# Four small edits to a hand-listed four-layer graph kernel: a bank rule for the list, one elu, one graph's row sums, the last stores' queue

## The chip, the cores and the metric

The kernel runs on one core of a Trainium2 chip. The metric is the time of one execution on the device in microseconds (us); the median over several runs is compared. All times below are measured on that chip: run times, or times of one execution recorded by the hardware profiler, counted from the start of its span.

## What is computed

Four layers run one after the other over 32 graphs of 512 nodes with 128 features each, all in float32, with one 0/1 adjacency matrix `adj` for all graphs. Every layer adds its result to x:

```python
h = relu(layernorm(x)); x = x + layer(h)
# layer 0: an edge-weighted message layer
x_h = elu(h @ Wi + bi)
e   = sigmoid(x_h @ We[H:] (target) + x_h @ We[:H] (source) + be) * mask(adj)
recv = elu(concat(e @ x_h, x_h * sum(e, -1)) @ Wn + bn)
out  = concat(recv, x_h) @ Wm + bm
# layer 1: five gated steps
av = concat(adj @ h, adj @ h); u3 = h @ u3_w.T
z, r = sigmoid(av @ w3.T + u3), sigmoid(av @ w4.T + u3)
h = (1 - z) * h + z * tanh(av @ w5.T + (r * h) @ u5.T)
# layer 2: adj @ (h @ W) + b
# layer 3: sum over k of adj^k @ h @ V[k], k = 0..3 (the two stacks of powers use the same adj)
```

## The kernel before

**Tiles.** A graph's activations are one tile of 128 partitions x 512 float32. Slots are pooled by kind: 36 `f` tiles in SBUF, 4 `q` tiles (rounded float32r copies), 8 small `s` tiles, 5 `x` tiles of four graphs each, 8 PSUM banks `b`, and DRAM scratch tiles `m` and `d`. Engines are named as in the profile: PE (matmul), DVE (VectorE), ACT (ScalarE), POOL (GpSimd), SP (SyncE, which issues most transfers).

**The order is made in advance.** The kernel does not emit instructions as it describes them. Each piece of work is registered with `op(engine, us, due, emit, reads, writes, ...)` (class `Plan`), with an assumed duration, a due time and the values it reads and writes. `Plan.op` derives what must come before it: the writer of each value read, and, for a value written, its earlier readers. `Plan.order` then goes through assumed time and picks for each engine the ready operation with the earliest due time; this list becomes the program, every engine runs its own part strictly in order, and semaphores are placed afterwards from what the instructions really read and write. So an entry that is changed anywhere can shift the places of all later ones.

**Start.** The first 18 us of the list (`BRANCH`) load x and adj, build the mask and fill PE with otherwise idle matmuls on ones (L307). Then a check whether adj is exact in float32r is read by all engines (L996), and one of two arms of an If is taken (L997). With these inputs it is the arm that splits a value into a rounded high part and the rest (`parts`, L821 on ACT and L825 on DVE).

**Layer 0** (`layer0`) for graph b: layernorm (L481 to L501), a turn into feature rows (PE for the first four graphs, L378 and L574), the product with Wi (L449), `elu`, the messages and scores (`send` L593 on PE; `score` L600 on DVE and `take` L598 on ACT read the same bank), the targets spread over partitions (L630), four tanh of edges (L645, ACT), each multiplied with the mask (L648, DVE), four products (L656), the row sums, `own` (L687), the product with Wn, a second `elu` and the product with Wm (L697), then the addition to x (L469).

`elu` reads one PSUM bank three times: exp (L554) and tanh (L454) on ACT, and the relu, on ACT (L562) or, for the first two graphs, on DVE (L559). DVE joins them (L564, L566).

Row sums: graphs 0 and 1 add the four edge tiles in pairs on DVE (L664) and sum over partitions with two float32 products on PE. All other graphs add the four tiles by transfers: SP copies the first into `sums` (L671) and POOL issues three accumulating transfers (L674), each after the one before has landed. ACT rounds the sum (L678), DVE takes the rest (L679) and PE sums both (L684).

**Layer 1** steps turn their result by DVE (L390), a write to DRAM (L392) and a read back (L403), both issued by SP, then `parts` and the products with adj (L851). **Layer 3** runs once for four graphs (`layer3`, products L932 and L941); its last round adds to x (L953, DVE) and stores each quarter (L958, issued by SP). The last quarter of the last four graphs is written to `mask` (L963) and stored after the If has ended (L1003, SP).

Of the kernel before, what the change touches and what calls it, by code (L numbers as in the profile page):

```python
# [14 lines left out]
ALU = mybir.AluOpType  # L15
# [26 lines left out]
class Plan:  # L42
# [18 lines left out]
    def op(self, eng, us, due, emit, reads=(), writes=(), two=None, keep=0, result=None,  # L61
           earliest=0.0, margin=0.0):

        two = eng == "POOL" if two is None else two
        o = Op(eng, us, self.RESULT[eng] if result is None else result, emit, two, keep)
        o.earliest, o.margin = earliest, margin
        for v in reads:  # L70
            o.before.add(v.writer)
        for v in writes:
            o.before.update(v.readers)
            if v.writer:
                o.before.add(v.writer)
            elif v.kind and v.slot is None:
                o.takes.append(v)
        for v in reads:
            v.readers.append(o)
        for v in writes:  # L80
            v.writer, v.readers = o, []
        o.vals = [v.whole or v for v in dict.fromkeys([*reads, *writes])]
        for v in o.vals:
            v.left += 1
        for v in [*reads, *writes, *o.vals]:
            self.vals[v] = True
        o.before -= {o, None}
        o.due = max([due, *(b.due for b in o.before)])
        for b in o.before:
            b.after.append(o)  # L90
        self.ops.append(o)
# [125 lines left out]
def tile_four_graph_layers(  # L217
# [27 lines left out]
    nc = tc.nc  # L245
    B, N, D = x.shape
    NC = N // P
    G = 4
    NG = B // G
# [5 lines left out]
    MARGIN = 10.0  # L255
    FIRST = 2

    T_MM, T_TR, T_NARROW, T_PASS = 0.86, 0.44, 0.224, 0.23
    T_VEC, T_COPY, T_ACT, T_DMA = 0.61, 0.5, 0.6, 0.45
# [3 lines left out]
    op = plan.op  # L263
# [20 lines left out]
    def at(v):  # L284
        if v.tile is not None:
            return v.tile
        return places[v.kind][v.slot] if v.whole is None else at(v.whole)[:, v.part]
# [262 lines left out]
    def elu(p, bias, half, due, keep, scale=1.0, relu_by_vector=False):  # L550


        e, t, r = Val("f"), Val("f"), Val("f")
        op("ACT", T_ACT, due, lambda: nc.scalar.activation(  # L554
            at(e), at(p), AF.Exp, bias=at(bias), scale=scale), [p, bias], [e], keep=keep)
        tanh(t, p, due, half, scale / 2)
        if relu_by_vector:
            assert scale == 1.0
            op("DVE", T_VEC, due, lambda: nc.vector.tensor_scalar(  # L559
                at(r), at(p), at(bias), 0.0, op0=ALU.add, op1=ALU.max), [p, bias], [r])  # L560
        else:
            op("ACT", T_ACT, due, lambda: nc.scalar.activation(  # L562
                at(r), at(p), AF.Relu, bias=at(bias), scale=scale), [p, bias], [r])
        op("DVE", T_VEC, due, lambda: nc.vector.scalar_tensor_tensor(  # L564
            at(t), at(e), 1.0, at(t), op0=ALU.add, op1=ALU.mult), [e, t], [t], two=True)
        op("DVE", T_VEC, due, lambda: nc.vector.scalar_tensor_tensor(  # L566
            at(r), at(t), 0.0, at(r), op0=ALU.min, op1=ALU.add), [t, r], [r], two=True)
        return r

    def layer0(b, h, due):  # L570
# [5 lines left out]
        else:  # L576
# [2 lines left out]
        pace = 0.6 if b < FIRST else 1.0  # L579
        d = due + 6 * pace  # L580
        xhT = elu(product(Wi_sb, hT, d, blocks=b >= G), bi_sb, bi_half, d, KEEP,
                  relu_by_vector=b < FIRST)

        d = due + 14 * pace
        msg, ends = Val("f"), Val("s")
# [22 lines left out]
        d = due + 20 * pace  # L608
# [33 lines left out]
        es = []  # L642
        for jc in range(NC):
            e = Val("f")
# [8 lines left out]
        d = due + 30 * pace  # L653
# [6 lines left out]
        if b < 2:  # L660
            ps = Val("b")
            pair = [Val("f"), Val("f")]
            for i in range(2):
                op("DVE", T_VEC, d - 6, lambda i=i: nc.vector.tensor_tensor(  # L664
                    at(pair[i]), at(es[2 * i]), at(es[2 * i + 1]), op=ALU.add),
                    [es[2 * i], es[2 * i + 1]], [pair[i]], two=True)
            for i in range(2):
                product(ones, pair[i], d - 1, ps, start=i == 0, stop=i == 1)
        else:
            sums = [Val("f")]  # L670
            op("SP", T_DMA, d - 10, lambda: nc.sync.dma_start(at(sums[0]), at(es[0])),  # L671
               [es[0]], [sums[0]], result=2.6)
            for e in es[1:]:
                op("POOL", 1.0, d - 10, lambda e=e: nc.gpsimd.dma_start(  # L674
                    at(sums[0]), at(e), accum_op=ALU.add), [e, sums[0]], [sums[0]],
                   two=False, result=4.6)
            high, low, ps = Val("q"), Val("q"), Val("b")
            op("ACT", T_COPY, d, lambda: nc.scalar.copy(at(high), at(sums[0])), [sums[0]], [high])  # L678
            op("DVE", T_VEC, d, lambda: nc.vector.tensor_tensor(  # L679
                at(low), at(sums[0]), at(high).bitcast(F32), op=ALU.subtract),  # L680
                [sums[0], high], [low], two=True)
            def total():
                for n, part in enumerate((low, high)):
                    nc.tensor.matmul(at(ps), at(ones_r), at(part), start=n == 0, stop=n == 1)  # L684
            op("PE", 2 * T_PASS, d, total, [high, low, ones_r], [ps])
# [6 lines left out]
        d = due + 44 * pace  # L692
# [43 lines left out]
    def list_rest(exact, pool):  # L736
        n = 25 if exact else 16
# [185 lines left out]
        def layer3(g, hT, due, pace):  # L923
            z = None
            for k in (3, 2, 1, 0):
                new = []
                for ic in range(NC):
                    d = due + ((3 - k) * NC + ic) * pace
                    pz = Val("b")
                    def start(pz=pz, k=k, ic=ic, last=z is None):  # L930
                        for i in range(G):
                            nc.tensor.matmul(  # L932
                                at(pz)[:, ts(i, D)], at(hT[i])[:, ts(ic, P)], at(V[k]),
                                start=i == 0, stop=last and i == G - 1,
                            )
                    op("PE", G * T_NARROW, d, start, [*hT, V[k]], [pz])
                    if z is not None:
                        for jc in range(NC):
                            def add(pz=pz, ic=ic, jc=jc, z=z[jc]):
                                for n, part in enumerate(z):  # L940
                                    nc.tensor.matmul(  # L941
                                        at(pz), at(adjT)[:, jc, ts(ic, P)], at(part),
                                        start=False, stop=jc == NC - 1 and n == PARTS - 1,
                                    )
                            op("PE", PARTS * T_ADJ, d, add, [*z[jc], adjT], [pz])
                    if k:
                        new.append(parts(pz, d))
                        continue
                    xv = X[g * G : (g + 1) * G]
                    def x_part(ic=ic):  # L950
                        return at(X_group[g])[:, :, ic, :]
                    def finish(pz=pz, x_part=x_part):
                        nc.vector.tensor_tensor(  # L953
                            x_part(), x_part(), at(pz).rearrange("p (b d) -> p b d", b=G),
                            op=ALU.add,
                        )
                    def store(ic=ic, x_part=x_part):
                        nc.sync.dma_start(  # L958
                            out[g * G : (g + 1) * G, ts(ic, P), :].rearrange("b p d -> p b d"),
                            x_part(),  # L960
                        )
                    if g == NG - 1 and ic == NC - 1:
                        op("DVE", T_VEC, d, lambda pz=pz, x_part=x_part: nc.vector.tensor_tensor(  # L963
                            at(mask)[:, 0, :].rearrange("p (b d) -> p b d", b=G), x_part(),
                            at(pz).rearrange("p (b d) -> p b d", b=G), op=ALU.add),
                            [pz, *xv], [mask])
                        continue
                    chunk = Val(whole=X_group[g])
                    op("DVE", T_VEC, d, finish, [pz, *xv], [chunk])

                    op("SP", 0.5, d, store, [chunk], margin=(NC - 1 - ic) * 2.7 + (g < NG - 1) * MARGIN)
                z = new


# [66 lines left out]
```

## Time and profile before

| what | us |
| --- | --- |
| runs | 1671.55, 1669.9, 1669.99; median 1669.99 |
| the profiled execution, own time | 1671.54 |
| its span, first to last instruction | 1669.4 |
| PE busy in the span | 1655.4 (99%) |
| DVE busy | 1428.0 (86%) |
| ACT busy | 1130.5 (68%) |
| POOL busy | 243.0 (15%) |

The busy time of PE counts overlapping matmuls once, and the ends of matmuls are modelled, so short gaps may be hidden in it. A graph's own path is long, but many graphs are under way at once: what counts is whether PE has something to do. The page shows PE at nine tenths or more in all of forty slices but the second and the last.

### The profile page before, as it was taken

To read this page: it belongs to the slowest core of one execution; us is meant where nothing else is said; L and a number is where in the kernel's file an instruction comes from. 1 tells how busy PE (TensorE), PEld (TensorE's weight loads), DVE (VectorE), ACT (ScalarE), POOL (GpSimd) and SP (SyncE) were. 2 spreads that over 40 slices of the span, in tenths; PEclk is the share of its full clock that TensorE was granted. 3 is DMA by queue.
4 is the path that set the end of the run, shared out by engine and by line. 5 is a ranking of instruction groups with operands and counts; after the bars stand their busy time and mean duration, and the time that the engine had idled before them with its cause. 6 is when DMAs were issued, how large, how long until landed. Compare 5 with 4: busy or idle time off the path is not lost.

```text
span 1669.4 us, 21469 instructions
## 1 busy us (share of the span) xinstructions
PE 1655.4 (99%) x6585; PEld 1072.9 (64%) x6585; DVE 1428.0 (86%) x3341; ACT 1130.5 (68%) x2133; POOL 243.0 (15%) x243
## 2 busy tenths in 40 slices
PE   9899999999999999999999999999999999999998
PEld 6555555656666666666666666666666666666787
DVE  8889999999998888889988898888999888877842
ACT  7876777877766677666667677676778666655640
POOL 2311101211111111111111111101121110000100
PEclk9999999999999999999999999999999999999999
DMA  3554524543445443454434454444454443222202
GB/s 98 128 121 127 151 88 123 147 123 110 136 111 145 117 115 103 107 148 122 121 112 108 121 139 115 114 113 126 128 140 127 127 122 100 89 64 87 84 14 59
DMA packets 285501, 189.10 MB, mean 113 GB/s; under 512 B 77376, under 2 KB 238016, under 8 KB 285376
## 3 DMA queue, kind: packets, MB, share of 16 engines
q1 hardware_dynamic: 272416, 164.03, 33.3%
q0 software_dynamic: 12960, 23.60, 8.5%
q8 instruction: 54, 0.88, 0.2%
q14 instruction: 71, 0.58, 0.1%
HBM read 82.78 MB, written 73.33 MB: 94 GB/s over the span
## 4 chain that ended last, share of the span: by engine, by line
PE 96%; DMA 1%; ACT 1%; DVE 1%; issue 0%; SPq 0%; DVEq 0%; ACTq 0%
PE b L449 44%; PE b L851 21%; PE b L941 11%; PE b L932 7%; PE b L656 6%; PE b L697 3%; PE b L914 2%; PE b L593 1%; PE b L684 1%; DMA f<-m 1%; ACT f L495 0%; PE b L307 0%; DMA f<-in_adj_dram 0%; DMA m<-f 0%; PE b L378 0%
## 5 line engine op out<-in xcount | busy, mean ns | idle before, releaser
L438 ACT COPY f<-b 128x512 f32<-128x512 f32 x356 | 206.6, 586 | 146.4 <-PE b L851 94.3
L851 PE MATMUL b<-AQ,r 128*128 128x512 f32 x1024 | 303.7, 438 | 0.0
L486 POOL TENSOR_TENSOR s<-s,nhalf 128x4 f32<-128x4 f32 x128 | 156.4, 1222 | 869.5 <-DVE s L484 793.0
L851 PEld LDWEIGHTS b<-AQ,r 128*128 128x128 f32 x1024 | 192.1, 188 | 89.2 <-issue 51.7
L876 DVE TENSOR_TENSOR f<-f,b 128x512 f32<-128x512 f32 x320 | 211.9, 676 | 25.5 <-PE b L449 23.3
L390 DVE STREAM_TRANSPOSE f<-f 128x512 f32<-128x512 f32 x246 | 207.3, 846 | 27.6 <-ACT f L495 27.1
L941 PE MATMUL b<-r,A_r 128*128 128x512 f32 x768 | 223.6, 426 | 0.0
L454 ACT ACTIVATE f<-f,b4w 128x512 f32<-128x512 f32 x160 | 115.0, 722 | 152.8 <-DVE f L876 152.4
L495 ACT ACTIVATE f<-x,s 128x128 f32<-128x128 f32 x504 | 206.9, 488 | 13.8 <-DVE s L490 13.4
L941 PEld LDWEIGHTS b<-r,A_r 128*128 128x128 f32 x768 | 139.0, 189 | 45.6 <-issue 23.4
L449 PE MATMUL b<-f,u3T 128*128 128x512 f32 x320 | 163.3, 592 | 2.4 <-DVE f L897 2.4
L449 PE MATMUL b<-f,u5T 128*128 128x512 f32 x320 | 162.9, 592 | 0.0
L449 PE MATMUL b<-f,w4T 128*128 128x512 f32 x320 | 162.9, 592 | 0.0
L449 PE MATMUL b<-f,w5T 128*128 128x512 f32 x320 | 162.7, 592 | 0.0
L449 PE MATMUL b<-f,w3T 128*128 128x512 f32 x320 | 162.2, 592 | 0.0
L674 POOL DMA_DIRECT2D f<-f x90 | 80.6, 896 | 486.9 <-DMA f<-f 94.6
L454 ACT ACTIVATE f<-b,b5w 128x512 f32<-128x512 f32 x160 | 109.7, 686 | 56.7 <-PE b L449 55.7
L851 PE MATMUL b<-A_r,r 128*128 128x512 f32 x512 | 147.5, 430 | 0.1
L893 DVE TENSOR_TENSOR f<-f,f 128x512 f32<-128x512 f32 x160 | 109.2, 683 | 43.0 <-ACT f L454 42.4
L932 PEld LDWEIGHTS b<-V,f 128*128 128x128 f32 x1024 | 131.1, 191 | 23.2 <-issue 17.7
L825 DVE TENSOR_TENSOR r<-f,r 128x512 fp32r<-128x512 f32 x192 | 130.4, 681 | 5.9 <-ACT r L821 5.9
L932 PE MATMUL b<-V,f 128*128 128x128 f32 x1024 | 133.1, 275 | 0.0
(111 smaller groups left out, 2526.2 us busy)
## 6 DMA issues: line engine op xcount, KB each, us to landing
m<-f SPq DMA_DIRECT2D x246, 256.0 KB, 2.1
f<-m SPq DMA_DIRECT2D x186, 256.0 KB, 3.0
f<-f POOLq DMA_DIRECT2D x90, 256.0 KB, 3.7
f<-m SPq DMA_DIRECT2D x240, 64.0 KB, 2.5
x<-in_x_dram SPq DMA_DIRECT2D x32, 256.0 KB, 3.3
out_dram<-x SPq DMA_DIRECT2D x31, 256.0 KB, 2.7
f<-f SPq DMA_DIRECT2D x30, 256.0 KB, 2.4
f<-d SPq DMA_DIRECT2D x28, 256.0 KB, 5.1
```

Of the source, the lines that this page charges most:

```text
L390: op("DVE", us, due, lambda: nc.vector.transpose(view_out(at(blocks)), view_in(at(src))), [src], [blocks])
L438: op("ACT", us, due, lambda: nc.scalar.copy(at(t), at(src)), [src], [t])
L449: nc.tensor.matmul(to, at(w), of, start=start, stop=stop)
L454: op("ACT", us, due, lambda: nc.scalar.activation(at(dst), at(src), AF.Tanh, bias=at(bias), scale=scale), [src, bias], [dst])
L486: op("POOL", 1.35, due, lambda: nc.gpsimd.tensor_tensor(stat(SCALE), stat(VAR), at(neg_half), op=ALU.pow), [s, neg_half], [s])
L495: nc.scalar.activation(at(h)[:, ts(c, P)], at(X[b])[:, c, :], AF.Relu, bias=stat(SHIFT)[:, c : c + 1], scale=stat(SCALE)[:, c : c + 1],)
L825: op("DVE", T_VEC, due, lambda: nc.vector.tensor_tensor(part(lo), whole(), part(hi).bitcast(F32), op=ALU.subtract), [src, hi], [lo], two=two)
L851: nc.tensor.matmul(at(pa), at(part)[:, ts(jc, P)], view(at(columns)[:, jc, :]), start=jc == n == 0, stop=jc == NC - 1 and n == PARTS - 1,)
L876: op("DVE", T_VEC, d, lambda: nc.vector.tensor_tensor(at(s), at(u), at(pg), op=ALU.add), [u, pg], [s])
L893: op("DVE", T_VEC, d, lambda c=c, h=h: nc.vector.tensor_tensor(at(c), at(c), at(h), op=ALU.subtract), [c, h], [c], two=True)
L932: nc.tensor.matmul(at(pz)[:, ts(i, D)], at(hT[i])[:, ts(ic, P)], at(V[k]), start=i == 0, stop=last and i == G - 1,)
L941: nc.tensor.matmul(at(pz), at(adjT)[:, jc, ts(ic, P)], at(part), start=False, stop=jc == NC - 1 and n == PARTS - 1,)
```

## The change

Four edits. (1) In `Plan.op`, an operation that reads a PSUM bank is also listed after the last earlier reader of the bank if that reader is on another engine. (2) The first `elu` takes its relu on ACT for all graphs. (3) The third graph (b = 2) adds its four edge tiles by three DVE additions in place of one SP and three POOL transfers. (4) The stores of the last four graphs' first three quarters are issued from ACT's queue. Two lines are added near the top, so the changed kernel's line numbers are 2 higher from there on and 8 or 9 higher after `layer0`'s sums (L851 becomes L859, L958 becomes L967).

```diff
@@ class Plan, op
         for v in reads:
             o.before.add(v.writer)
+            if v.kind == "b" and v.readers and v.readers[-1].eng != eng:
+                o.before.add(v.readers[-1])
         for v in writes:
@@ layer0
         xhT = elu(product(Wi_sb, hT, d, blocks=b >= G), bi_sb, bi_half, d, KEEP,
-                  relu_by_vector=b < FIRST)
+                  relu_by_vector=False)
@@ layer0, row sums of graphs 2 and up
             sums = [Val("f")]
-            op("SP", T_DMA, d - 10, lambda: nc.sync.dma_start(at(sums[0]), at(es[0])),
-               [es[0]], [sums[0]], result=2.6)
-            for e in es[1:]:
-                op("POOL", 1.0, d - 10, lambda e=e: nc.gpsimd.dma_start(
-                    at(sums[0]), at(e), accum_op=ALU.add), [e, sums[0]], [sums[0]],
-                   two=False, result=4.6)
+            if b < 3:
+                for n in range(1, NC):
+                    op("DVE", T_VEC, d - 10, lambda n=n: nc.vector.tensor_tensor(
+                        at(sums[0]), at(es[0] if n == 1 else sums[0]), at(es[n]), op=ALU.add),
+                        [es[n], es[0] if n == 1 else sums[0]], [sums[0]], two=True)
+            else:
+                ...
@@ layer3, last round
-                        nc.sync.dma_start(
+
+                        (nc.scalar if g == NG - 1 else nc.sync).dma_start(
                             out[g * G : (g + 1) * G, ts(ic, P), :].rearrange("b p d -> p b d"),
                             x_part(),
                         )
@@
-                    op("SP", 0.5, d, store, [chunk], margin=(NC - 1 - ic) * 2.7 + (g < NG - 1) * MARGIN)
+                    op("ACT" if g == NG - 1 else "SP", 0.5, d, store, [chunk], margin=(NC - 1 - ic) * 2.7 + (g < NG - 1) * MARGIN)
```

The branch marked `...` holds the SP and POOL transfers as they were.

## The prediction

> **What bounds the kernel now.** First the page: the engine totals and the chain that ended last.
>
> ```profile
> PE 1655.4 (99%) x6585; PEld 1072.9 (64%) x6585; DVE 1428.0 (86%) x3341; ACT 1130.5 (68%) x2133; POOL 243.0 (15%) x243
> PE 96%; DMA 1%; ACT 1%; DVE 1%; issue 0%; SPq 0%; DVEq 0%; ACTq 0%
> ```
>
> PE carries the chain. The change removes no matmul of the work, so it can only win time in which PE does nothing useful. The table by stretches (span, then each engine's busy time, then the granted clock) shows where that is:
>
> ```profile
> core 0: us, PE busy (x) PEld busy (x) DVE busy (x) ACT busy (x) POOL busy (x), PEclk, DMA share, GB/s
> 28.20:31.62 3.42, 1.45 (x10) 0.85 (x9) 2.95 (x14) 3.42 (x10) 0.82 (x1) 1.00 0.00 0
> 31.62:35.03 3.41, 3.41 (x18) 3.41 (x18) 2.16 (x11) 2.45 (x6) 1.90 (x2) 0.50 0.00 0
> 72.58:75.99 3.41, 1.72 (x5) 0.41 (x3) 3.11 (x5) 3.41 (x7) 0.86 (x1) 1.00 0.58 135
> 20.00:100.00 80.00, 73.26 (x287) 44.37 (x286) 66.60 (x179) 64.53 (x132) 24.09 (x30) 0.98 0.43 107
> 100.00:1640.00 1540.00, 1539.29 (x6028) 990.90 (x6027) 1339.54 (x3104) 1050.59 (x1973) 214.75 (x199) 1.00 0.42 114
> ```
>
> PE idles 80 - 73.26 = 6.7 us between 20 and 100 us and 0.7 us in the next 1540. One stretch of 3.41 us ran at half clock: 1.7 us more. The first 20 us wait for loads and fillers; the end is a store. The waits of PE itself name the opening's causes, and the timeline of the end shows the last one:
>
> ```profile
> PE b L449 <- DVE f L897: 2.4, 1, 2.4
> PE b L449 <- DMA f<-m: 2.1, 2, 1.5
> PE b L697 <- DVE f L566: 2.0, 2, 1.2
> ...
> 1661.34 0.69 DVE L953 TENSOR_TENSOR x<-x,b 128x512 f32<-128x512 f32 x1 [1.13 <-PE b L941]
> ...
> 1664.06 0.69 DVE L963 TENSOR_TENSOR mask<-x,b 128x512 f32<-128x512 f32 x1 [2.03 <-PE b L941]
> 1665.65 0.38 SPq L1003 DMA_DIRECT2D out_dram<-mask  x1
> ```
>
> The last store is issued at 1665.65, though its data stand at 1664.06 + 0.69 = 1664.75. The store of the quarter before was issued at 1662.06, 0.03 us after its data (1661.34 + 0.69). Its issue ended at 1662.43; SP needed 3.2 us to get out of the If.
>
> **What the Trainium skill says.** "PSUM - Partial Sum Buffer", section on bank collisions: two engines may not access one bank at once, reads included, so software keeps them apart. The trace agrees: exp (ACT L554) waited 0.5 us for the relu (DVE L559) that only reads the same bank. "TensorE: Matmul & The Clock Gate", Part 1: the clock is full or half, set by how busy PE was in windows of 3413 ns. The trace agrees: one window at 0.50, after one in which PE was busy 1.45 of 3.42 us; 1.72 of 3.41 us (at 72.58) brought no half clock. "DMA: Bandwidth & Descriptors", Issuing engines are not separate DMA queues: issuing elsewhere saves only the issuer's time; that is how I price the ACT stores. "Advanced Engine Details and Errata", Control Flow Timing, gives a branch as about 51 ns; SP's 3.2 us are far from it, and the measurement decides.
>
> **Part by part.** *Stores on ACT.* SP's last work in the arm becomes the fourth-last store, issued at about 1655.7; 0.37 + 3.2 us later, at 1659.3, it stands behind the If and waits for the data. The last store then goes at 1664.75 + 0.03 = 1664.78: 0.87 us gained. In the changed order nothing stands behind the three stores on ACT but its own jump. The trace has no transfer issued by ACT; taken as SP's 0.37 us, ACT is out at 1662.06 + 0.37 + 3.2 = 1665.6, ahead of the landing at 1664.78 + 2.7 = 1667.5. Bounds: 0.9 gained; nothing, if the join fetches late again; 1 us lost, if a first transfer from ACT takes 2 us more than SP's. I take 0.87.
>
> *Relu on ACT, and the bank rule at the start.* ACT's changed order for graph 0 is exp, relu, tanh. Exp starts at 10.96 (end of L531) and not 11.56, but relu (0.57) goes before tanh, which ends at 12.79 as before (12.82): no gain for graph 0. DVE loses 0.75 us, and the layernorm of graph 1 (L501, 1.1 us) moves from 16.86 to about 11.7. So graph 1's product with Wi runs at 15.7 (20.5 before), its elu is joined at 24.2 (26.7). The price: ACT does graph 1's exp ahead of graph 0's edges, and graph 0's product with Wn moves from 26.1 to about 26.9.
>
> I went through the changed order from there with the rows' step times (DVE 128x512 0.60, ACT 0.57, copies 0.5, layernorm on ACT 1.55, a float32 product 0.86). To compare progress I subtract from the start of a product the work that PE has behind it (0.86 per float32 product, 0.23 per float32r, 0.22 per L593 or L697 product, 0.11 per transpose): the rest is lost time.
>
> - Before: 13.9 us are lost when the first L656 starts, 20.0 at graph 0's L851 (52.8), 22.4 at its second step (79.4), 24.5 at its L449 with w4T at 97.8.
> - After: 14.2 at the first L656 (20.1). Then three waits: 2.4 us near 30 to 32 (an L839 product needs the bank that the tanh of graph 1's edges reads until 32.2), 1.9 near 43 (graph 3's turned rows sit on ACT behind a layernorm and the second elu), 0.6 in small ones. 18.6 at graph 0's L851.
> - In the changed order PE has graph 2's Wi and a first L656 early, so the window before 31.6 holds about 1.65 us of PE work in 3.41, between the 1.45 that brought half clock and the 1.72 that did not. I take full clock; with half clock 1.3 us of the lead go.
>
> *Third graph's sums on DVE.* Before, SP's L671 is issued at 47.93, POOL's L674 at 50.89, 55.08 and 59.05, and ACT takes the sum at 67.66: 19.7 us. Three DVE additions of 0.60, among graph 0's and graph 1's work, give it at about 53, and ACT rounds it at once. Price: 1.8 us of DVE, 1.5 of which the two relus left free. SP is spared one issue, POOL three of 0.9 us. The third graph's Wn, Wm and layer 1 come about 13 us earlier (L687's product at 59 and not 72.4), into the stretch of 70 to 84 us where PE now idles 2.4 and 1.5 us. There the changed order leaves about 1.3 us at the first L851 on turned rows (L390 ends at 67.4, then transfers of 2.1 and 3.0, copy and subtraction, with queueing until 75.9), and 0.6 at L593: 20.5 lost at 88 us.
>
> So the opening gains 24.5 - 20.5 = 4.0 us. These hand-offs are timed without queueing at the semaphores, so I take off 0.6: 3.4.
>
> *The bank rule later.* In 40 of 64 places DVE's score now waits for ACT's take; in the changed order it never does, and ACT stands behind DVE instead, by one DVE operation (0.6 us) at most. ACT has 1669 - 1130 = 539 us idle, so I cost it at nothing; uncovered it would be 64 x 0.6 = 38 us.
>
> Sum: 3.4 + 0.87 = 4.3 us. The profiled execution stands 1.55 us above the median (1671.54, its span 1669.4 and 2.1 around it), so it would go to 1667.2 and the median to 1665.7.
>
> **The rivals.** *Lead not kept*: the window near 30 us falls to half clock (1.3 us back), and the lead is lost to waits of the kind above, each 1 to 2 us, since 66.6 of 80 us of DVE are full there. Only the end's 0.9 is left: 1669.1. For it: the windows' 1.65 is close to 1.45. Against: the 14 us that the sums come earlier do not depend on it. *ACT behind DVE* (slower): if more than a third of the 64 takes delay their L656 by 0.6 us with nothing else ready on PE, that is 12.8 us, less 4.3: 1678.5. It is slower by over 0.2% (3.3 us, about what a measurement of this kernel can tell from no change) from 13 of 64 on. Against: PE idles 0.7 us in 1540. For it: a new list moves every operation, and no trace shows it. *The change does not reach the path*: a list that simply idles elsewhere by as much gives 1670 with the end lost too.
>
> **How the numbers follow.** Forecast (opening gain between 1.5 and 7 us): 0.6, of which 0.05 is within 0.2%. Lead not kept or not reached: 0.27, nearly all within 0.2%. ACT behind DVE, or later waits of that size: 0.13, of which 0.01 within. So faster 0.55, same 0.33, slower 0.12. The range goes from 1662.0 (the end's 0.87 and 7.1 of the 8.4 us that idling and half clock take in the opening) up to 1672.0, which leaves out most of the slower case.
>
> **What would show it.** After: PE's idle time in 20 to 100 us 1 to 4 us smaller; graph 2's L692 near 57 us; no half clock near 32 to 35; the last store issued within 0.1 us of its DVE add; PE's idle in the middle still below 2 us. Wrong, if a half-clock window or a wait over 2 us stands in the opening, if the last store still trails its data by 0.9, or if PE waits on L656 in the middle.

## The result and the profile after

The changed kernel takes 1674.0 us, median of 18 runs (1671.5 to 1674.66); the kernel before, run beside it on the same chip, 1670.62 us (1669.32 to 1673.17). The ratio is 1.0018, 95% interval 1.0011 to 1.0025: some 3 us slower, where 4.3 us faster was forecast. The profiled execution of the changed kernel took 1672.98 us; its span is 1671.2 us, 1.8 longer than before. What lies outside the span is about 2.1 us in the runs of the kernel before and 1.8 in those of the changed one, so the two profiled executions themselves differ by 1.4 us.

First the page of the changed kernel, the engine totals and the chain that ended last, by engine:

```profile
PE 1655.0 (99%) x6579; PEld 1072.0 (64%) x6579; DVE 1428.7 (85%) x3342; ACT 1130.2 (68%) x2135; POOL 242.6 (15%) x240
PE 94%; DVE 2%; ACT 1%; DMA 1%; issue 0%; SPq 0%; DVEq 0%
```

The work is the same but for six of the idle matmuls at the start (92 before, 86 now); PE still carries the chain. So the difference is in when PE works, at what clock, and in what comes after it. The table by stretches of the changed kernel (columns as in its first line):

```profile
core 0: us, PE busy (x) PEld busy (x) DVE busy (x) ACT busy (x) POOL busy (x), PEclk, DMA share, GB/s
28.74:32.16 3.42, 1.70 (x5) 0.51 (x4) 3.18 (x14) 3.42 (x7) 2.35 (x2) 1.00 0.01 2
32.16:35.57 3.41, 3.02 (x7) 1.89 (x8) 2.94 (x5) 3.41 (x10) 0.00 (x0) 0.50 0.00 0
20.00:100.00 80.00, 72.61 (x281) 43.06 (x282) 67.43 (x175) 64.41 (x132) 19.39 (x26) 0.98 0.33 89
100.00:1640.00 1540.00, 1539.29 (x6029) 991.09 (x6028) 1339.71 (x3103) 1049.61 (x1975) 218.49 (x201) 1.00 0.42 114
```

The middle is untouched: 0.71 us of PE idle in 1540, as before. In 20 to 100 us PE idles 80 - 72.61 = 7.4 us, where before it was 6.7; one to four less was forecast. The half-clock stretch is still there, right after a stretch in which PE was busy 1.70 of 3.42 us. The waits of PE (engine, who it waited for: total, times, longest), and the timeline of the end:

```profile
PE b L451 <- ACT f L576: 2.1, 1, 2.1
PE b L847 <- ACT f L647: 1.8, 1, 1.8
PE b L451 <- DMA f<-m: 1.5, 1, 1.5
PE b L859 <- DVE r L833: 1.2, 1, 1.2
...
1662.27 0.69 DVE L961 TENSOR_TENSOR x<-x,b 128x512 f32<-128x512 f32 x1 [1.13 <-PE b L949]
...
1664.99 0.69 DVE L972 TENSOR_TENSOR mask<-x,b 128x512 f32<-128x512 f32 x1 [2.03 <-PE b L949]
1665.70 0.38 SPq L1012 DMA_DIRECT2D out_dram<-mask  x1
```

The causes shown in the list of waits are new except the third. At the end, the last store is issued 0.02 us after its data stand (1664.99 + 0.69 = 1665.68), as forecast. But look when it lands, that is, when its data have arrived and its completion is signalled. The view of that line gives the time from issue to landing; the DMA view of two stretches of the end tells the packets by queue (packets, MB, share of 16 DMA engines), first 1666.5 to 1668.6, then 1668.4 to 1669.8:

```profile
DMA to landing us min/median/max: 4.3/4.3/4.3
...
q1 hardware_dynamic: 496, 0.25, 39.9%
q8 instruction: 1, 0.02, 5.3%
...
q1 hardware_dynamic: 33, 0.02, 5.6%
```

The same view of that store in the kernel before (L1003):

```profile
DMA to landing us min/median/max: 2.7/2.7/2.7
```

Queue q1 carries the store: 528 packets, 33 for each of 16 DMA engines (one packet lies in both stretches). The first 15 shares have landed by 1668.18 us; one share, 33 packets in 0.02 MB, goes out only afterwards and lands at 1670.04, both by the times of the completion signals in the trace. Ahead of it, by the packets' own times, stands one packet of the queue "instruction", 16 KB, from 1666.81 to 1668.60 (5.3% of 16 engines in 2.1 us is 1.78 us).

### The profile page after: what moved, and what is told of

Same layout as the page of the kernel before. It is cut to its first block, busy times and chain, and to the rows that moved or that the text cites. A ratio compares the mean times of both kernels' runs of the same rounds, so it can differ in the third digit from the quotient of the medians.

```text
span 1671.2 us, 21455 instructions
## 1 busy us (share of the span) xinstructions
PE 1655.0 (99%) x6579; PEld 1072.0 (64%) x6579; DVE 1428.7 (85%) x3342; ACT 1130.2 (68%) x2135; POOL 242.6 (15%) x240
## 4 chain that ended last, share of the span: by engine, by line
PE 94%; DVE 2%; ACT 1%; DMA 1%; issue 0%; SPq 0%; DVEq 0%
PE b L451 43%; PE b L859 20%; PE b L949 11%; PE b L940 7%; PE b L658 6%; PE b L705 3%; PE b L922 2%; PE b L595 1%; PE b L692 1%; DMA m<-f 1%; ACT f L497 1%; DMA f<-m 0%; DVE f L392 0%; DMA f<-in_adj_dram 0%; DVE f L903 0%
## 5 line engine op out<-in xcount | busy, mean ns | idle before, releaser
L859 PE MATMUL b<-AQ,r 128*128 128x512 f32 x1024 | 303.9, 438 | 1.2 <-DVE r L833 1.2
L859 PEld LDWEIGHTS b<-AQ,r 128*128 128x128 f32 x1024 | 192.0, 188 | 90.3 <-issue 50.2
L859 PE MATMUL b<-A_r,r 128*128 128x512 f32 x512 | 149.6, 434 | 0.0
L456 ACT ACTIVATE f<-f,b3w 128x512 f32<-128x512 f32 x160 | 114.8, 719 | 33.3 <-DVE f L884 32.3
```

Of the source, the lines that this page charges most:

```text
L456: op("ACT", us, due, lambda: nc.scalar.activation(at(dst), at(src), AF.Tanh, bias=at(bias), scale=scale), [src, bias], [dst])
L859: nc.tensor.matmul(at(pa), at(part)[:, ts(jc, P)], view(at(columns)[:, jc, :]), start=jc == n == 0, stop=jc == NC - 1 and n == PARTS - 1,)
```

## The experiments

Each kernel ran beside the kernel before on the same chip; the ratio is to that, with its 95% interval. 0.001 is 1.67 us. The medians of the kernel before lay between 1669.6 and 1670.8 us, so ratios are safer to compare than medians. Three theories at the start: *fetch* (a sixteenth of the last store waits for the instructions that TensorE fetches as it leaves the If), *queue* (the ScalarE queue makes it late), *opening* (the end won its 0.87 us, and the loss is all in the list).

### The end

**Stores alone, and stores taken back.** The diff of the fourth edit, on the kernel before and undone in the changed kernel:

```diff
-nc.sync.dma_start(
+(nc.scalar if g == NG - 1 else nc.sync).dma_start(
-op("SP", 0.5, d, store, ...)
+op("ACT" if g == NG - 1 else "SP", 0.5, d, store, ...)
```

> The kernel before with the last three stores on ScalarE's queue and nothing else; TensorE, VectorE and GpSimd have the same lists. Fetch theory: last store issued 0.9 us earlier, its data then meet TensorE's fetch (1665.6 to 1666.8 in the trace before), one landing of sixteen is late: landing 3.5 to 4.5 us after the issue and the time 0 to 1 us longer than before, about 1671.1. Queue theory: landing near 4.3 us whatever TensorE fetches, about 1671.4. Opening theory: 0.87 us faster, about 1669.7.

Measured: 1670.35 us, 0.9996 (0.9988 to 1.0004). The landing took 4.0 us.

> The changed kernel with its last three stores back on SP's queue; the rest of its list is the same. Fetch theory (one sixteenth of the last store waits behind the 16 KB of instructions that TensorE fetches after its exit from the If): the store is issued 0.9 us later, its piece behind the fetch ends at about 1669.3 instead of 1670.0, so 0 to 0.7 us faster than the changed kernel, about 1673.5. Queue theory (ScalarE's queue makes the landing slow): landing 2.7 us after the issue again, about 0.7 us faster too. Opening theory (the end kept its 0.87 us of gain and the loss is all ahead of 100 us): 0.9 us slower than the changed kernel, about 1674.9.

Measured: 1673.19 us, 1.0018 (1.0009 to 1.0028). The landing took 2.8 us. So the stores alone are worth nothing that can be measured, and without them the changed kernel is as slow: the bulk of its loss is in the list. The times alone don't tell fetch from queue.

**Moving TensorE's exit.** Five matmuls that nobody reads, after the list of each arm (the profile counts each of these float32 matmuls twice, so they appear as x10):

```diff
             issue(plan.order())
+            for _ in range(5):
+                nc.tensor.matmul(places["b"][plan.free["b"][0][1]][:, :P], at(ones), at(ones), start=True, stop=True)
```

> The kernel before with the same five matmuls at the end of each arm. Fetch theory: the fetch moves from 1665.6 to about 1666.7, into the last store's data, as in the changed kernel: landing about 4.3 us after the issue instead of 2.7, and the time 1 to 1.7 us longer than before, about 1672.0. Queue theory and opening theory: no difference, about 1670.6, since SP issues every store and TensorE's extra work lies behind the last add.

Measured: 1671.23 us, 1.0005 (0.9997 to 1.0013), too close to call by time. But with every store on SP and nothing added but PE's five matmuls, the landing went from 2.7 to 3.7 us.

> The changed kernel with five more matmuls of 128x128 at the very end of each arm of the If, into a bank that nobody reads: TensorE leaves the If some 1.1 us later, and so does its fetch. Fetch theory: the fetch begins near 1667.9, when the last store's data have passed; landing about 2.4 us after the issue instead of 4.3, and the time 1 to 1.9 us shorter than the changed kernel, about 1672.3, though TensorE does more. Queue theory: landing stays near 4.3 us, the time the same. Opening theory: the same.

Measured: 1672.46 us, 1.0009 (1.0001 to 1.0017), with a landing of 2.5 us: by the ratios about 1.5 us faster than the changed kernel, with more work on PE. The two intervals overlap; the landing, 1.8 us sooner, is the clearer sign.

The cleanest pair came later, on edits 3 and 4 together, without and with the five matmuls. In both traces the last add begins within 0.02 us of the same time. Without them, the timeline, then the DMA view of 1661.5 to 1663.85 and of 1663.85 to 1665.4:

```profile
1660.68 0.69 DVE L969 TENSOR_TENSOR mask<-x,b 128x512 f32<-128x512 f32 x1 [2.03 <-PE b L947]
1661.39 0.38 SPq L1009 DMA_DIRECT2D out_dram<-mask  x1
...
q1 hardware_dynamic: 495, 0.25, 36.0%
out_dram<-mask SPq DMA_DIRECT2D x1, 256.0 KB, 4.2
...
q1 hardware_dynamic: 33, 0.02, 5.2%
```

And with them, the timeline and the DMA view of the first of these stretches (in the second, no packet of q1 is left):

```profile
1660.50 1.27 PE L742 MATMUL b<-ones 128*128 128x128 f32 x10
1660.70 0.69 DVE L971 TENSOR_TENSOR mask<-x,b 128x512 f32<-128x512 f32 x1 [2.03 <-PE b L949]
1661.42 0.38 SPq L1011 DMA_DIRECT2D out_dram<-mask  x1
...
q1 hardware_dynamic: 528, 0.26, 37.5%
out_dram<-mask SPq DMA_DIRECT2D x1, 256.0 KB, 2.4
```

All 528 packets against 495: one share of sixteen is the whole difference. By the packets' times the 16 KB fetch began at 1662.38 us without the five matmuls and at 1663.68 with them, and the store's data pass from 1662.3 to 1663.4 where nothing holds them up. So it is in all six traces in which a share is late: its first packet begins within 0.03 us of the fetch's end (1664.16 and 1664.18 us here, 1668.58 and 1668.60 in the changed kernel). And in all eighteen traces the fetch begins 1.4 to 2.0 us after PE's last matmul, and it moves when that matmul moves: it is PE's. The ends of all traces in one table, those of the later kernels too; "from last add" runs from the add's start to the landing of the last share:

| kernels | first three quarters stored by | issue to landing, us | from last add, us |
| --- | --- | --- | --- |
| before | SP | 2.7 | 4.25 |
| eight others | SP | 2.3 to 2.8 | 3.95 to 4.42 |
| before, five matmuls | SP | 3.7 | 5.31 |
| changed | ACT | 4.3 | 5.05 |
| four others | ACT | 3.6 to 4.2 | 4.29 to 4.96 |
| changed, five matmuls | ACT | 2.5 | 3.23 |
| two others with five matmuls | ACT | 2.4, 2.6 | 3.11, 3.36 |

The queue theory is out: the landing follows PE's exit, whichever engine issued the stores, and the transfers from ACT themselves landed in 2.6 us (median). In the traces edit 4 wins its 0.9 us of issue and loses as much or up to twice that at the landing (in time, alone, no difference is measured); only with the exit delayed is it a gain, about 1 us from the last add.

"Runtime: NRT & Kernel Launch" in the Trainium skill, section Instruction fetch mechanics, says that instructions are fetched in blocks of 16 KiB, 256 instructions, and that a taken branch out of the fetched window forces a fetch by DMA. The trace agrees: this queue moved 54 packets of 16 KB, and PE's 2 x 6579 matmuls and weight loads make 51.4 blocks of 256. That such a block delays a share of somebody's store the page does not say; the runs show it.

### The list: which edit, and where

> The kernel before with edit 2 alone (graphs 0 and 1 take their first elu's relu on ScalarE too). Elu theory (this edit sets the order ahead of the If and puts the waits for ScalarE there, 2.1 us for graph 3's f by L576 and 1.8 us for the bank that graph 1's tanh of L647 reads): 2 to 3 us slower than before, about 1673, with those waits in the trace. Rule theory: no difference, about 1670.8. Sums theory: no difference. Sum-of-small-things theory (every new order of the list lands somewhere within a microsecond or two, and no edit owns the loss): within 1.5 us of before either way.

Measured: 1672.25 us, 1.0015 (1.0008 to 1.0021).

> The kernel before with edit 1 alone (a reader of a bank on another engine is counted as waiting for the reader ahead of it). Elu theory: no difference to before, about 1670.8. Rule theory (the list now issues scores after takes, holds TensorE's products back behind them, and the waits at bank turns in the changed kernel come from that): 2 to 3 us slower, about 1673. Sums theory: no difference. Sum-of-small-things theory: within 1.5 us either way.

Measured: 1673.68 us, 1.0018 (1.0010 to 1.0026).

> The kernel before with edit 3 alone (graph 2's sums by three VectorE additions instead of four transfers). Sums theory (about 1.8 us more of VectorE near 60 us make its rows late for TensorE, the 1.2 us of L859 for DVE r and the 0.9 us of L658): 1 to 2.5 us slower than before, about 1672.5. Elu and rule theories: 0 to 1 us faster than before, as predicted for this edit, about 1670.3. Sum-of-small-things theory: within 1.5 us either way.

Measured: 1668.86 us, 0.9993 (0.9985 to 1.0001).

> The changed kernel without edit 1: edits 2, 3 and 4. Elu theory: as the changed kernel, about 1673.5 to 1674. Rule theory: the loss of the opening goes, about 1670.5 with the end as in the kernel with edit 4 alone. Sums theory: as the changed kernel. Sum-of-small-things theory: anywhere from 1670 to 1674.

Measured: 1673.43 us, 1.0020 (1.0013 to 1.0026).

Edits 1 and 2 each lose 2.5 to 3 us alone, and not 5.5 together: both theories are half right. The waits named for the elu theory were not in its trace (there PE waited 1.7 us for ACT L562 and 1.6 for DVE L566), so the loss does not need those two hand-offs; what is left is the new order. The sums theory is out: edit 3 costs nothing and by its median wins 1.2 us, with an interval that touches zero.

The next two put the rule's condition under a flag, set for all groups of four graphs but the first (shown), or for the first alone (`g == 0`, and set from the start):

```diff
-            if v.kind == "b" and v.readers and v.readers[-1].eng != eng:
+            if self.turns and v.kind == "b" and v.readers and v.readers[-1].eng != eng:
...
+            plan.turns = g > 0
```

> The kernel before with the rule of edit 1 from the second group of four graphs on; the first group's list is made as before. Opening theory (all that the rule costs lies between 30 and 60 us, where TensorE runs dry; from 100 us on it has always other work): no difference to before, about 1670.3. Everywhere theory (the rule orders the products of every graph less well, or makes a half-clock stretch likelier at any place): 1 to 3 us slower, about 1672.

Measured: 1671.0 us, 1.0006 (0.9998 to 1.0015).

> The kernel before with the rule of edit 1 in the first group of four graphs alone. Opening theory: the whole loss of the kernel with edit 1 alone, 2.5 to 3.5 us slower than before, about 1673.4, with TensorE busy near 25.3 of the 30 us from 30 to 60 instead of 28.0, and its waits for DVE f L566 (1.7 and 1.6 us). Everywhere theory: 1 to 1.5 us slower, about 1671.6.

Measured: 1673.74 us, 1.0023 (1.0016 to 1.0030).

> The kernel before with edits 1 and 3. If effects add (3.0 us lost by edit 1, 1.2 us won by edit 3 alone): about 1672.0. If edit 3 wins only in the order of the kernel before, since it fills a gap at 60 to 100 us that edit 1 has already shifted to 30 to 60 us (TensorE busy 38.6 of 40 there with edit 1, 36.1 before): about 1673.5.

Measured: 1671.98 us, 1.0014 (1.0006 to 1.0023).

The rule loses its time in the first group; for 28 graphs it costs at most 2.5 us by its interval and perhaps nothing. Edit 3 keeps about 0.7 us of its 1.2 on top of the rule, which the intervals cannot tell from either expectation.

PE's idle time in the traces, 20 to 60 and 60 to 100 us (40 less its busy time):

| kernel | 20 to 60 | 60 to 100 | sum | mean granted clock of its runs |
| --- | --- | --- | --- | --- |
| before | 2.9 | 3.9 | 6.8 | 0.9986 to 0.9991 |
| edit 1 alone | 5.3 | 1.4 | 6.7 | 0.9976 |
| edit 2 alone | 4.9 | 1.1 | 6.0 | 0.9981 |
| edit 3 alone | 3.0 | 0.5 | 3.5 | 0.9988 |
| changed | 4.6 | 2.8 | 7.4 | 0.9984 |

Edits 1 and 2 do not idle longer in sum; they idle earlier, in a few long waits between 28 and 48 us. Yet they take 2.5 to 3 us more. What differs besides is the clock of their runs: while PE is busy, 0.001 of it is 1.67 us. Half clock after the end of PE's work costs nothing and is in these means too (0.0012 in the trace of the changed kernel, 0.0008 in that of before), so they are a hint and no sum.

A single trace is no firmer. The kernel before, with edit 4 alone, and with the five matmuls alone have the same order of work up to the end. Yet their traces show half clock from 31.62 us on, from 83.91 us on, and nowhere before the end, and their last add begins at 1664.06, 1665.22 and 1663.37 us. The windows of the clock do not stand at the same places either: from 31.62 to 83.91 us are 15.3 windows of 3.41 us. So one stretch of half clock in one trace is not a property of the kernel, and a difference of 1 or 2 us between two single traces does not price a list.

### The list: waits that cost twice

So the open question was how much of the loss is waiting and how much the half clock that follows. The next kernels fill the waits with matmuls that do nothing:

```diff
-            issue(plan.order())
+            nc.gpsimd.memset(at(zeros), 0.0)
+            issue(padded(plan.order(), {19: (4, 19, False), 20: (6, 20, True), 30: (6, 30, False), 32: (2, 32, True)}))
```

`padded` emits, ahead of PE's operation 19 of the arm, four matmuls of ones into the bank of operation 19, and so on; `True` adds ones x zeros to a bank already started. For the changed kernel it is `{19: (6, 21, True), 34: (8, 34, False)}` (six ahead of operation 19 into the bank of 21, and so on).

> The kernel with the rule in the first group alone, and TensorE kept busy in its four waits of 28 to 48 us: 4, 6, 6 and 2 matmuls of 128x128 (some 0.22 us each) ahead of the products that waited 1.09, 1.68, 1.58 and 0.67 us. They write a bank that the waiting product starts anew, or add zeros to one; the output's values don't change. Clock theory (the waits cost twice: as waits, and since they bring a second stretch of 3.4 us at half clock, at 46.9 us in the trace of the kernel without them): no half-clock stretch or one alone, granted clock 0.999 or 1.000 instead of 0.998, and 1.2 to 3 us faster than 1673.7, though TensorE does 18 matmuls more. Idle theory (the lost time is the waits alone): no difference, 1673.5 to 1674.5, whatever the clock.

Measured: 1670.79 us, 1.0007 (0.9999 to 1.0015), mean granted clock 0.9997, against 1.0023 (1.0016 to 1.0030) and 0.9980 without. The intervals don't meet: about 2.7 of the 3.8 us are back, with 18 matmuls more. Here are the stretches of the kernel without the filling, then of the one with it, in windows of 3.41 us as the clock of the first had them, and the first one's waits between 28 and 48 us:

```profile
29.87:33.28 3.41, 0.64 (x4) 0.43 (x4) 2.86 (x12) 3.41 (x7) 1.54 (x2) 1.00 0.00 0
33.28:36.69 3.41, 3.41 (x17) 3.39 (x17) 2.78 (x6) 1.38 (x6) 0.52 (x1) 0.50 0.00 0
43.52:46.93 3.41, 1.62 (x10) 0.97 (x8) 2.62 (x5) 3.41 (x7) 0.00 (x0) 1.00 0.35 111
46.93:50.34 3.41, 2.95 (x14) 2.98 (x15) 0.58 (x3) 3.41 (x10) 0.00 (x0) 0.50 0.29 86
...
PE b L700 <- DVE f L569: 1.7, 1, 1.7
PE b L596 <- DVE f L569: 1.6, 1, 1.6
PE b L758 <- ACT f L565: 1.1, 1, 1.1
PE b L700 <- DVE s L603: 0.7, 1, 0.7
```

```profile
29.87:33.28 3.41, 2.32 (x21) 2.08 (x20) 2.63 (x12) 3.41 (x8) 1.55 (x2) 1.00 0.00 0
33.28:36.69 3.41, 3.41 (x24) 2.73 (x24) 3.41 (x6) 1.61 (x6) 0.74 (x1) 1.00 0.00 0
43.52:46.93 3.41, 2.80 (x23) 2.42 (x22) 2.74 (x6) 3.41 (x8) 0.00 (x0) 1.00 0.38 121
46.93:50.34 3.41, 3.41 (x26) 2.85 (x25) 1.70 (x5) 3.41 (x10) 0.00 (x0) 1.00 0.24 71
```

Read the second column and the clock in pairs of lines. Without the filling, PE is busy 0.64 us in one window, and the next runs at 0.50; it is busy 1.62 us in another, and the next runs at 0.50. With it both are over 2.3 us, and the clock stays at 1.00 (the second trace's own windows stand 0.41 us later; there PE is busy 2.48 and 2.81 us). The full-speed windows did more products: x24 and x26 against x17 and x14, fillers included. This is "TensorE: Matmul & The Clock Gate", Part 1 in the Trainium skill (the clock follows the activity of windows of 3413 ns), which the prediction used, and the trace agrees. It does not yield a sharp limit in busy time. In the changed kernel 1.70 us busy brought half clock, but two other windows of the same trace read:

```profile
45.81:49.22 3.41, 1.68 (x9) 1.20 (x10) 2.50 (x4) 3.41 (x8) 0.00 (x0) 1.00 0.62 193
49.22:52.64 3.42, 3.42 (x18) 2.08 (x17) 3.42 (x7) 3.42 (x8) 0.00 (x0) 1.00 0.04 16
```

Here 1.68 us busy is followed by full clock; with the end's matmuls 1.57 us (from 90.34) is too, and 1.54 (from 28.90) is not.

> The changed kernel with its two longest waits filled likewise: 6 matmuls ahead of the product that waited 1.81 us for graph 1's tanh, 8 ahead of the one that waited 2.14 us for graph 3's f. Clock theory: granted clock 0.999 or more instead of 0.998, 1 to 2 us faster than the changed kernel's 1674.0. Idle theory: no difference.

Measured: 1672.37 us, 1.0016 (1.0009 to 1.0022), mean granted clock 0.9993. By the ratio it is 0.3 us better than the changed kernel, within the noise, though the clock rose as expected. So in the changed kernel it is not shown that the list's time goes into half clock; the two intervals would still leave room for a gain of 1.3 us.

The reason that its trace suggests: the half-clock stretch of the changed kernel holds 7 matmuls and waits of PE anyway, while that of the kernel with the rule holds 17, so the slow clock has little to slow. This is argued from the trace, not tried.

> The changed kernel with its two longest waits filled, as in the run before, and the five matmuls at the end of each arm. If the half clock of the opening (1.6 us by the kernel with the waits filled) and the late landing (1.5 us by the kernel with the end's matmuls) are the loss, and they add: 1670.9, about 3.1 us faster than the changed kernel and within 1.5 us of the kernel before. If one of the two gains was chance, or the two are the same: 1672.4.

Measured: 1671.38 us, 1.0008 (0.9999 to 1.0016), every run at a granted clock of 1.000. That is what the end's five matmuls gave alone (1.0009). The end's repair is seen twice (the intervals of each pair overlap, but the landing falls to 2.5 and 2.6 us); the filling's is not seen. What is left of the list against the kernel before is 0.0008, some 1.3 us, with an interval that touches zero.

### A version that beats both

> Edits 3 and 4 on the kernel before, without the matmuls at the end of the arms. Fetch theory: the last store's data meet TensorE's fetch, landing 3.6 to 4.3 us after the issue, so the end is worth nothing: 0.8 to 1.9 us slower than the kernel with those matmuls, about 1669.3. If the matmuls do nothing: 1668.0.

Measured: 1668.67 us, 0.9995 (0.9986 to 1.0003). In time it is not told apart from the next one; in the trace the landing is, as shown above.

> Edits 3 and 4 alone on the kernel before, and five matmuls of 128x128 at the end of each arm that nobody reads, to have TensorE's fetch of instructions after the last store's data. Fetch theory: the list of the kernel with edit 3 alone (1.0 to 1.2 us faster than before), and the 0.87 us of the end that edit 4 wins once no landing waits for the fetch: landing near 2.5 us after the issue, about 1668.2 where before is 1670.3. If the end is worth nothing: about 1669.2.

Measured: 1668.02 us, 0.9989 (0.9983 to 0.9996), mean granted clock 0.9998: 1.8 us faster than the kernel before and, by the ratios, 4.8 us faster than the changed kernel. Its opening, from its table by stretches:

```profile
20.00:60.00 40.00, 37.27 (x162) 22.27 (x161) 36.02 (x114) 35.07 (x77) 12.27 (x19) 1.00 0.21 61
60.00:100.00 40.00, 39.50 (x138) 22.66 (x137) 35.29 (x81) 32.32 (x61) 8.87 (x11) 1.00 0.56 133
```

PE idles 3.2 us there and does not fall to half clock in this execution.

## Why the prediction was wrong

Two terms of "3.4 + 0.87 = 4.3 us" failed. The larger is the opening's 3.4 us: edits 1 and 2 were priced as a lead, and each of them alone made the kernel 2.5 to 3 us slower. The smaller is the end's 0.87 us, which alone gained nothing that can be measured. By its size, 0.18%, the result falls into the prediction's case of a change within 0.2%, which had a chance of 0.33.

**The end: the issue right, the landing wrong.** The issue came 0.02 us after the data, as worked out. The step that failed is "ahead of the landing at 1664.78 + 2.7": the 2.7 us was carried over from a store that was issued 0.9 us later, when PE's fetch was nearly past. It measured 4.3. So 0.87 us to be won became 5.05 - 4.25 = 0.8 us lost in the traces. The lower bound of 1 us lost was the right size for the wrong reason: transfers from ACT were not slow. The trace before held the clue. SP's 3.2 us on the way out of the If was read as a price of SP alone; PE leaves the same If, and its 16 KB fetch stands in that trace from 1665.56 to 1666.80 us, just where an earlier store would go.

**Half clock: the wrong choice at the edge.** The prediction had the window ahead of 32 us at 1.65 us of PE work, between 1.45 and 1.72, and wrote "I take full clock". It measured 1.70, and half clock followed. Such a limit is not in the traces (1.68 us in the same trace brought none), and where the windows fall differs from execution to execution, so the choice could only be given a chance. For this kernel filling the waits gave nothing measurable, though the priced 1.3 us is not excluded; for edit 1 in the first group the waits' half clock is most of the loss.

**The opening: most of the waits right, the sum wrong.** The waits foreseen were 2.4 us for graph 1's tanh, 1.9 for graph 3's rows, 1.3 for the turned rows and 0.6 at L593; measured are 1.8, 2.1, 1.2 and 0.2. Not foreseen is 1.5 us at 92.4 us, where PE waits for rows read back from DRAM. It lies just past the place where the counting stopped ("20.5 lost at 88 us"); the "before" was counted to 97.8. With that wait and the half clock at its priced 1.3 us, 4.0 us of gain are about 1.2. Measured, PE's idle time from 20 to 100 us grew by 0.7 us and the last add came 0.9 us later. The step that failed is "Relu on ACT, and the bank rule at the start": the lead that it was to bring did not last, and each of the two loses 2.5 to 3 us alone. The prediction's own signs of being wrong, a half-clock window and a wait over 2 us in the opening, both came (2.1 us for graph 3's rows).

**The third graph's sums: right in kind, 3 us late.** The timeline of the changed kernel has them, on DVE, ACT and PE:

```profile
49.91 0.69 DVE L675 TENSOR_TENSOR f<-f,f 128x512 f32<-128x512 f32 x1
53.52 0.68 DVE L675 TENSOR_TENSOR f<-f,f 128x512 f32<-128x512 f32 x1
55.38 0.68 DVE L675 TENSOR_TENSOR f<-f,f 128x512 f32<-128x512 f32 x1
56.27 0.62 ACT L686 CAST q<-f 128x512 fp32r<-128x512 f32 x1
59.52 1.02 PE L692 MATMUL b<-q,ones_r 128*128 128x512 f32 x2
```

The sum stands at 56.1 us where about 53 was written, and 67.7 before; the product follows at 59.5 instead of 57. Alone the edit gains 1.2 us (interval -0.2 to 2.5), and PE's idle from 60 to 100 us falls from 3.9 to 0.5.

**The bank rule later: not contradicted.** PE idles 0.71 us in the middle in both kernels, and the rule without its first group is at 1.0006 (0.9998 to 1.0015), so a cost of up to 2.5 us is not excluded.

**From one trace to a median.** The working set the profiled execution 1.55 us above the median of three runs (0.9 above that of all 18) and gave the changed kernel the same distance. Its own profiled execution lies 1.0 us *below* its median, so 1.4 us of difference in the two profiled executions stand for 3.4 in the medians. The rival nearest in mechanism is *Lead not kept*; its 1669.1 was low by the end's lost gain and by what edits 1 and 2 cost. No rival let the end itself get slower, and the range stopped 2.0 us short.

**Still open.** The changed kernel's list loses more in times (end on SP: 1.0018) than its trace explains: the last add begins 0.9 us later in the changed kernel's trace and 1.7 later with the end on SP, for the same list; with the waits filled it begins at 1665.36 and, with the end's matmuls added, at 1663.97. How the loss divides between PE's waits and clock stretches that differ from run to run isn't settled, nor is why edit 2 alone, whose trace has no more half clock than that of before, is slower.

## What to carry to other kernels

Price an idle time of PE by where it falls: a window of 3.4 us with half of it busy or less can halve the clock of the next one (here 0.64 to 1.70 us busy did, 1.57 to 1.68 in other windows did not), so a few matmuls that do nothing may win more than the wait itself, if there is dense work after it. An end that leaves a branch is shared by all engines: look for instruction fetches among the packets of the last store before pricing an earlier issue, and note that delaying an exit can be the gain. Measure the parts of a bundled change alone: here the one edit that shortened a chain of transfers did not lose and probably won, and two reorderings that looked like a lead each lost more. And compare lists by many runs: traces of one order of work alone differed by 1.9 us at the last add.

## What the runs showed that was not expected

- A 16 KB instruction fetch of PE held up one sixteenth of a 256 KB store by up to 1.9 us (15 shares landed by 1668.18, the last at 1670.04).
- Five idle matmuls at the end of PE's program cut 1.8 us from a traced span (1666.8 to 1664.9 us, with the last add at the same time).
- Eighteen idle matmuls in four waits cut the time by about 2.7 us; the two windows at half clock of the trace without them were gone.
- In one trace 1.70 us busy in a window of 3.41 us was followed by half clock and 1.68 us in another window was not; and traces of the same order of work had half clock at different places or not at all.
